# Image 0 of a two-layer fp32 block: when the sums of weight tiles run on after a pause

## The chip, the cores and the metric

The kernel runs on one core of one Trainium2 chip. The metric is the device time of one execution in microseconds; of several runs the median is taken.

## The reference

Eight images of 384 channels and 32 x 32 positions pass through two layers, in fp32. The first is a transformer block on 1024 tokens, the second a ConvNeXt-like block:

```python
# layer 0: xf is (8, 1024, 384)
qkv  = layernorm(xf, g1, beta1) @ w_qkv.T + b_qkv         # 8 heads of 48
out  = softmax(q @ k.T * 48**-0.5) @ v
x1   = out @ w_proj.T + b_proj + xf
y    = x1 + gelu(layernorm(x1, g2, beta2) @ w_fc1.T + b_fc1) @ w_fc2.T + b_fc2   # hidden 1536
# layer 1
y    = depthwise_conv_7x7(x) + dw_b
y    = layernorm(y over channels) * ln_w + ln_b
y    = gelu(y @ w1 + b1)                                  # hidden 1536
gx   = sqrt(sum over positions of y**2);  nx = gx / (mean over channels of gx + 1e-6)
y    = grn_gamma * (y * nx) + grn_beta + y
out  = x + y @ w2 + b2
```

## The kernel before, in words

Images go one after the other. TensorE does, for each: q and k, values, attention in two halves of 512 queries (for each of four pairs of heads eight steps of scores and products), the projection of each half, fc1, fc2; the depthwise convolution of an image is done on VectorE (with some taps by ScalarE and GpSimd) while TensorE works on the next image.

**Fewer matmuls through sums of tiles.** From image 1 on, q and k, w1 and (for most images) fc1, and from image 0 on fc2, are computed with a scheme that multiplies sums of weight tiles with sums of input tiles. The sums of the weights do not depend on the image. They are made once, while image 0 runs, and stored in DRAM (`s_qk`, `s_w1`, `s_fc1`, `s_fc2`, `s_w2`), from where the later products load them. Biases that a norm's or a GRN's shift adds are folded in the same time.

**The planner.** The program is recorded in Python. `Flow` holds a clock of TensorE's time at record time: each recorded group of matmuls adds its nominal length (`flow.pe`). Side work is written as generators ("chains"); a chain that yields a number is resumed when that much TensorE time has been recorded. So a yield decides behind which matmul the next instructions of the chain stand in their engine's queue. On the chip each engine takes its queue in order and waits at each instruction for its semaphores. `flow.finish` runs the rest of a chain at once.

**The side chains of image 0**, spawned before its attention except for fc1's:

- `sums_for_tiles(i)`, i = 0 and 1, starting 33 and 38 us after the spawn: three times `sums_singly`, for a third of q/k's, then w1's tiles. Both chains work in the free columns of the big `qk` tile. Each `sums_singly` issues a load of 128 x 1920 on GpSimd's queue (L1593), yields, makes 18 VectorE operations of 128 x 128 in nine groups (L1600 additions, L1603, L1637 and L1638 negations), and stores the tile by GpSimd (L1640).
- `sums_for_fc1`, after image 0's attention: two more `sums_singly`, in the tile `v`.
- `prepare(weights, False)`: fc2's sums (`forms`, L1661 to L1698; operations of 128 x 512 at L1651, L1654, L1683, L1692, L1694, stores at L1669), then `shift_through_w2` (b2's shift), then w2's sums by the same `forms`. All three use the one buffer of tag `acc`, so each load of the next waits for the last reader of the one before. `shift_through_w2` has three rounds: two loads (L1746, tile `w_gbeta`), two products on VectorE (L1752, 128 x 768), an addition (L1755), five additions (L1759), a column sum on TensorE (L294, tile `b` in a bank of the scores' pool, which has two) and a copy on ScalarE (L1763).
- `prepare(weights, True)`: b1's shift (L1725, L1727 on `pad`).

**What runs on the main path.** After the last pair of heads in each half the sums of the softmax are inverted and spread: `average` copies (L777, ScalarE), adds (L779, VectorE), moves the sums by SyncE's DMA, inverts (L786, VectorE), moves the inverses back by SyncE, and multiplies (L805, VectorE) once they have landed (tile `r`); then the projection (L760) reads the result. Then the norm before fc1: sums of channels on VectorE (L551, L554), a matmul with ones (L518, `ln_sum`), subtraction (L561), squares on ScalarE (L568), their addition (L572, L575), a matmul (L518, `ln_var`), Ln and Exp on ScalarE (L588, L589), scaling (L594). For the first half of the queries this norm runs between the attention steps of the second half.

**The pause.** When the first half has nine steps left to go, the list `quiet` gets an entry, and it is cleared behind the projection; the same again at the end of the second half. While `quiet` holds something, a chain that comes to `pause()` yields 1.0, up to 24 times, and then goes on:

```python
def pause():
    for _ in range(24):
        if quiet:
            yield 1.0
```

Chains 0 and 1 of the sums, and `shift_through_w2`, thus resume at the same TensorE time, and their groups come in turn.

**fc2** (`by_thirds`, L496) is 15 products of four matmuls each. Its inputs are made on VectorE between the products (L1083, pairs of 128 x 1024), its results are added to the image at L1080 and L1083.

Of the kernel before, what the change touches and what calls it, by code (L numbers as in the profile page):

```python
# [176 lines left out]
def block_kernel(  # L177
# [90 lines left out]
    def col(name, i):  # L268
        at, width = VEC[name]
        assert i < width  # L270
        return vec[:, at + i : at + i + 1]
# [20 lines left out]
    def column_sums(ps, i, weights, rows=slice(0, P)):  # L292

        nc.tensor.matmul(out=ps[rows, i : i + 1], lhsT=weights, rhs=ones[:, 0:1], start=True, stop=True)  # L294
        flow.pe(0.2)
# [13 lines left out]
    def columns(name):  # L309
        at, width = VEC[name]  # L310
        return vec[:, at : at + width]
# [38 lines left out]
    def chunk(w, c):  # L350
        return w[:, c * 6 * P : (c + 1) * 6 * P]
# [1227 lines left out]
            column_sums(ps, ct, t[:, ct * P : (ct + 1) * P])  # L1579
        nc.vector.tensor_tensor(bout, ps[:, :CT], columns("bproj"), ALU.add)  # L1580

    def pause():
        for _ in range(24):
            if quiet:
                yield 1.0

    def sums_singly(w, store, spare):

        shape = store.shape
        t = spare[:, : shape[1] * shape[2] * P].rearrange("p (g n o) -> p g n o", n=shape[2], o=P)
        nc.gpsimd.dma_start(out=t, in_=w.rearrange("p (g n o) -> p g n o", n=shape[2], o=P))  # L1593
        yield 13.0
        yield from pause()
        r = {n: t[:, :, i, :] for i, n in enumerate(SINGLY)}
        a12, a13, a21, a22, a23, a31, a32, a33 = (r[n] for n in (12, 13, 9, 4, 14, 0, 3, 10))

        def plus(dst, one_, other, op=ALU.add):
            nc.vector.tensor_tensor(dst, one_, other, op)  # L1600

        def minus(dst, one_, other):
            nc.vector.scalar_tensor_tensor(dst, one_, -1.0, other, ALU.mult, ALU.subtract)  # L1603

        plus(r[6], r[6], a12)
        plus(r[14], a23, a33)
        yield 0.6
        yield from pause()
        minus(r[5], r[6], a33)
        plus(r[8], r[6], a13)  # L1610
        yield 0.6
        yield from pause()
        plus(r[8], r[8], r[14], ALU.subtract)
        plus(r[11], r[14], a12, ALU.subtract)
        yield 0.6
        yield from pause()
        plus(r[13], a13, a12, ALU.subtract)
        plus(r[13], r[13], a33, ALU.subtract)
        yield 0.6
        yield from pause()  # L1620
        plus(r[7], r[14], a22, ALU.subtract)
        plus(r[4], a21, a22)
        yield 0.6
        yield from pause()
        plus(r[2], a33, r[4], ALU.subtract)
        plus(r[4], r[4], a31)
        yield 0.6
        yield from pause()
        plus(r[1], a32, r[4])
        minus(r[9], a21, a12)  # L1630
        yield 0.6
        yield from pause()
        plus(r[9], r[9], a31, ALU.subtract)
        plus(r[0], a31, r[6], ALU.subtract)
        yield 0.6
        yield from pause()
        nc.vector.tensor_scalar(r[12], a12, -1.0, None, ALU.mult)  # L1637
        nc.vector.tensor_scalar(r[14], r[14], -1.0, None, ALU.mult)  # L1638
        yield 1.0
        nc.gpsimd.dma_start(out=store, in_=t)  # L1640

    def prepare(weights, aside):
# [3 lines left out]
        def blocks(name):  # L1646
            t = one.tile([P, CT, N], F32, tag="acc", name=name).rearrange("p c n -> p (c n)")
            return t.rearrange("p (j k o) -> p j k o", j=4, o=P)
# [93 lines left out]
        def shift_through_w2():  # L1742
            for r in range(CT):
                t = blocks(f"w2_gbeta_{r}")
                for s in range(2):
                    nc.gpsimd.dma_start(out=t[:, s], in_=chunk(w2, 2 * r + s).rearrange("p (k o) -> p k o", o=P))  # L1746
                yield 14.0
                h = HT // 2
                for s in range(2):
                    yield from pause()  # L1750
                    g = columns("gbeta")[:, s * h : (s + 1) * h].unsqueeze(2).to_broadcast((P, h, P))
                    nc.vector.tensor_tensor(t[:, s], t[:, s], g, ALU.mult)  # L1752
                    yield 1.0
                yield from pause()
                nc.vector.tensor_tensor(t[:, 0], t[:, 0], t[:, 1], ALU.add)  # L1755
                for k in range(1, h):
                    yield 0.5
                    yield from pause()
                    nc.vector.tensor_tensor(t[:, 0, 0, :], t[:, 0, 0, :], t[:, 0, k, :], ALU.add)  # L1759
                yield 7.0  # L1760
                ps = ps_s.tile([P, N], F32, tag="s", name=f"b2_{r}")
                column_sums(ps, 0, t[:, 0, 0, :])
                nc.scalar.activation(b2[:, r : r + 1], ps[:, :1], AF.Identity, bias=col("b2", r), scale=1.0)  # L1763
# [7 lines left out]
        def release():  # L1771
            yield 14.0
            weights.release()

        yield from forms("fc2", wfc2, s_fc2)
        flow.spawn(release())
        yield 8.0
        yield from shift_through_w2()
        yield from forms("w2", w2, s_w2)

# [86 lines left out]
    def main():  # L1867
# [81 lines left out]
        def sums_for_tiles(i):  # L1949
            width = len(FORMS) * P  # L1950
            spare = large[0][:, (2 * NP + 2 * i) * N : (2 * NP + 2 * i + 2) * N]
            for w, store, g in ((wqkt, s_qk, i), (w1t, s_w1, i), (w1t, s_w1, i + 2)):
                yield from sums_singly(w[:, g * width : (g + 1) * width], store[:, g : g + 1], spare)
                yield 8.0

        def sums_for_fc1():
            width = len(FORMS) * P
            spare = v.rearrange("p t w -> p (t w)")
            for g in range(2):
                yield from sums_singly(wfc1t[:, g * width : (g + 1) * width], s_fc1[:, g : g + 1], spare)  # L1960
                yield 8.0
            for t in range(KT):
                nc.gpsimd.memset(v[:, t, :], 1.0)
# [122 lines left out]
        for b in range(B):  # L2086
            if b == 0:
                folding = flow.spawn(after(None, folds(weights), 8))
                preparing = flow.spawn(after(None, prepare(weights, False), 4))
                singly = [flow.spawn(after(None, sums_for_tiles(i), 33 + 5 * i)) for i in range(2)]  # L2090
                aside = flow.spawn(after(folding, prepare(weights, True), 4))
# [4 lines left out]
            if b == 0:  # L2096
                for chain in singly:
                    flow.finish(chain)
                fc1_sums = flow.spawn(after(None, sums_for_fc1(), 22.0))
                shift = flow.spawn(after(None, prepare(weights, None), 4.0))  # L2100
# [204 lines left out]
```

## Time and profile before

| | us |
|---|---|
| median of 3 runs | 3212.09 (3211.55 to 3214.67) |
| the profiled execution | 3213.02 |
| its span, first to last instruction | 3211.1 |
| TensorE busy | 3196.2 (100% of the span) |
| VectorE busy | 2550.4 (79%) |
| ScalarE busy | 1674.6 (52%) |
| GpSimd busy | 493.4 (15%) |
| mean granted TensorE clock | 0.999 |

Image 0 takes about the first 324 us: q, k and v to 67, attention to 191 with the first projection at 134.73 to 142.7, fc1 and the second projection to 269, fc2 to 324. The profile's times count from the first instruction. A row of a timeline gives start, duration, engine, source line, operation, tiles written and read, shapes, the number of instructions merged into it, and in brackets the engine's idle time before it with what ended that. TensorE's busy time contains waits too short for the profile to list.

### The profile page before, as it was taken

Reading aid. Unit: us, or ns where it says so; the run is one execution under the profiler, and the core shown is the slowest. Engines: PE = TensorE matmul, PEld = TensorE weight load, DVE = VectorE, ACT = ScalarE, POOL = GpSimd, SP = SyncE. Lnnn points to the kernel's source line nnn. Section 1 sums busy time; section 2 is a strip of 40 time slices with the busy share of each in tenths; the row PEclk is TensorE's granted clock in tenths of the full one; section 3 lists DMA queues with packets and bytes.
Section 4 is the critical chain, followed back from the end, with each engine's and each line's share of the span. In section 5 each row is a group of like instructions: output and inputs, shape, how many; then the busy total and the mean of one; then the engine's idle time right before and its main releaser. Section 6 shows DMA issues by size and latency. Waiting matters only on the chain.

```text
span 3211.1 us, 39348 instructions
## 1 busy us (share of the span) xinstructions
PE 3196.2 (100%) x14204; PEld 1402.1 (44%) x14204; DVE 2550.4 (79%) x3587; ACT 1674.6 (52%) x2363; POOL 493.4 (15%) x592
## 2 busy tenths in 40 slices
PE   9999999999999999999999999999999999999999
PEld 5344434443444434444344443444435444344454
DVE  4547788897878978789787888888887788879964
ACT  3542763456644476444754637637365374732543
POOL 2102211112111121201112011120111201200000
PEclk9999999999999999999999999999999999999999
DMA  6435742647346564456546374463743638433244
GB/s 210 155 127 170 168 90 50 162 112 165 84 88 159 123 151 92 97 142 158 115 92 124 116 186 97 81 136 106 194 92 80 148 97 200 72 81 93 55 119 111
DMA packets 206052, 393.09 MB, mean 122 GB/s; under 512 B 42656, under 2 KB 48416, under 8 KB 205472
## 3 DMA queue, kind: packets, MB, share of 16 engines
q0 software_dynamic: 79296, 163.35, 26.6%
q1 hardware_dynamic: 126272, 226.49, 23.6%
q8 instruction: 114, 1.87, 0.2%
q10 hardware_dynamic: 288, 0.71, 0.1%
q14 instruction: 82, 0.67, 0.1%
HBM read 212.98 MB, written 40.11 MB: 79 GB/s over the span
## 4 chain that ended last, share of the span: by engine, by line
PE 97%; DVE 1%; DMA 1%; ACT 0%; issue 0%; SPq 0%; DVEq 0%; ACTq 0%
PE fc L415 15%; PE s L818 13%; PE o L838 13%; PE o_p L496 11%; PE fc_p L496 11%; PE v L738 4%; PE proj L760 4%; PE h_n L467 3%; PE h_z L467 3%; PE h_x L467 3%; PE h_last L1427 2%; PE o L1378 2%; PE h L402 2%; PE qk_n L467 2%; PE qk_z L467 2%; PE qk_x L467 1%
## 5 line engine op out<-in xcount | busy, mean ns | idle before, releaser
L1244 DVE SCALAR_TENSOR_TENSOR acc<-pad,vec,acc 128x870 f32<-128x870 f32 (+8 forms) x815 | 911.0, 1157 | 2.7
L827 ACT ACTIVATE p<-s 128x1024 f32<-128x1024 f32 x512 | 524.3, 1025 | 255.2 <-PE s L818 246.9
L818 PE MATMUL s<-qk 48*64 48x512 f32 x4096 | 538.7, 591 | 0.4 <-ACT qk L660 0.2
L838 PE MATMUL o<-p,v 64*64 64x512 f32 x4096 | 535.7, 589 | 0.0
L1280 POOL DMA_DIRECT2D acc<-tap x266 | 227.0, 859 | 1354.9 <-ACT tap L1279 647.5
L415 PE MATMUL fc<-xn,fc 128*128 128x512 f32 x972 | 427.7, 594 | 0.1
L496 PE MATMUL o_p<-y,w 128*128 128x512 f32 x664 | 289.0, 592 | 0.0
L838 PEld LDWEIGHTS o<-p,v 64*64 64x64 f32 x4096 | 166.4, 132 | 273.3 <-issue 265.0
L415 PEld LDWEIGHTS fc<-xn,fc 128*128 128x128 f32 x972 | 183.1, 190 | 229.2 <-issue 220.5
L818 PEld LDWEIGHTS s<-qk 48*64 48x64 f32 x4096 | 162.3, 132 | 275.9 <-issue 213.1
L496 PE MATMUL fc_p<-qk,fc 128*128 128x512 f32 x520 | 226.6, 593 | 0.3 <-DMA qk<-qk 0.3
L1279 ACT ACTIVATE tap<-pad,vec 128x512 f32<-128x512 f32 x266 | 195.1, 736 | 2.9 <-DMA acc<-tap 2.9
L496 PEld LDWEIGHTS o_p<-y,w 128*128 128x128 f32 x664 | 125.6, 190 | 157.7 <-issue 146.4
L1244 DVE SCALAR_TENSOR_TENSOR acc_last<-pad,vec,acc_last 128x377 f32<-128x377 f32 (+24 forms) x288 | 177.2, 688 | 0.6
L496 PEld LDWEIGHTS fc_p<-qk,fc 128*128 128x128 f32 x520 | 98.2, 190 | 126.9 <-issue 117.4
L508 ACT ACTIVATE qk<-fc,bfc_f 128x512 f32<-128x512 f32 x90 | 61.6, 685 | 160.4 <-PE fc L415 160.4
L508 ACT ACTIVATE hid<-fc,bfc_f 128x512 f32<-128x512 f32 x72 | 49.4, 687 | 158.3 <-PE fc L415 158.3
L779 DVE TENSOR_TENSOR attn<-o,attn 128x512 f32<-128x512 f32 x64 | 44.1, 689 | 109.9 <-ACT attn L777 108.8
L760 PE MATMUL proj<-attn,wproj_sb 128*128 128x512 f32 x288 | 127.5, 596 | 0.7 <-DVE attn L805 0.7
L738 PE MATMUL v<-wv_sb,xn 128*128 128x384 f32 x384 | 126.8, 487 | 0.0
L991 ACT COPY pad<-x 128x512 f32<-128x512 f32 x42 | 26.3, 634 | 187.7 <-DVE x L1083 187.7
L738 PEld LDWEIGHTS v<-wv_sb,xn 128*128 128x128 f32 x384 | 72.5, 190 | 50.1 <-issue 3.4
(446 smaller groups left out, 4594.7 us busy)
## 6 DMA issues: line engine op xcount, KB each, us to landing
acc<-tap POOLq DMA_DIRECT2D x266, 256.0 KB, 3.5
fc<-s_fc SPq DMA_DIRECT2D x91, 256.0 KB, 3.0
w<-s_w SPq DMA_DIRECT2D x91, 256.0 KB, 2.7
w<-s_w SPq DMA_DIRECT2D x72, 320.0 KB, 4.2
fc<-in_wfc SPq DMA_DIRECT2D x54, 384.0 KB, 4.0
y<-y POOLq DMA_DIRECT2D x38, 512.0 KB, 6.7
qk<-qk POOLq DMA_DIRECT2D x30, 512.0 KB, 9.4
qk<-s_qk SPq DMA_DIRECT2D x42, 320.0 KB, 4.9
```

Source lines behind the costliest of these rows:

```text
L415: nc.tensor.matmul(out=ps, lhsT=lhsT(k), rhs=rhs(k)[:, half(h)], start=(k == 0), stop=(k == nk - 1))
L467: nc.tensor.matmul(out=at, lhsT=weights.at(wname, g, slot // 5)[:, slot % 5, :], rhs=rhs[n], start=first, stop=True, skip_group_check=not ...
L496: nc.tensor.matmul(out=bank, lhsT=lhsT, rhs=rhs, start=k == 0, stop=k == len(pairs) - 1)
L508: nc.scalar.activation(dst, src, function, **kw)
L738: nc.tensor.matmul(out=ps[:, :C], lhsT=xn[:, k, t * P : (t + 1) * P], rhs=wv_sb[:, k, :], start=(k == 0), stop=(k == CT - 1),)
L760: nc.tensor.matmul(out=ps, lhsT=wproj_sb[:, m, ct * P : (ct + 1) * P], rhs=attn[:, m, :], start=(m == 0), stop=(m == CT - 1),)
L818: nc.tensor.matmul(out=s[64 * i : 64 * i + 64, j, :], lhsT=kT[64 * j : 64 * j + HD, m, k0 : k0 + 64], rhs=qT[64 * j : 64 * j + HD, m, half ...
L827: nc.scalar.activation(p, s, AF.Exp)
L838: nc.tensor.matmul(out=outs[i][64 * j : 64 * j + 64, :], lhsT=v[keys, t, at : at + 64], rhs=p[keys, j, :], start=(t == 0), stop=(t == KT - 1),
L1244: nc.vector.scalar_tensor_tensor(dst, window, tap, dst, ALU.mult, ALU.add)
L1279: nc.scalar.mul(t.rearrange("p (h w) -> p h w", w=W), window, tap)
L1280: nc.gpsimd.dma_start(out=acc[:, ct, half(h)], in_=t, accum_op=ALU.add)
```

## The change

Four edits, all in the planning of image 0's side chains:

- `pause` takes a number. A chain that was in fact held yields this number once more when the pause ends, so that it resumes later. `sums_singly` hands it on: 11 for chain 0 of the q/k and w1 sums, 16 for chain 1. For fc1's sums and in `shift_through_w2` it is 0, a yield that lets other due chains go first.
- `sums_singly` yields 10 us instead of 13 between its load and its first operation.
- `shift_through_w2` yields 12 us instead of 14 between its loads and its first product.
- Between fc2's sums and `shift_through_w2` 3 us are yielded instead of 8.

```diff
-    def pause():
+    def pause(behind=0):
+        paused = False
         for _ in range(24):
             if quiet:
+                paused = True
                 yield 1.0
-
-    def sums_singly(w, store, spare):
+        if paused:
+            yield behind
+
+    def sums_singly(w, store, spare, behind=0):
...
         nc.gpsimd.dma_start(out=t, in_=w.rearrange("p (g n o) -> p g n o", n=shape[2], o=P))
-        yield 13.0
-        yield from pause()
+        yield 10.0
+        yield from pause(behind)
...
         plus(r[6], r[6], a12)
         plus(r[14], a23, a33)
         yield 0.6
-        yield from pause()
+        yield from pause(behind)
...
                     nc.gpsimd.dma_start(out=t[:, s], in_=chunk(w2, 2 * r + s).rearrange("p (k o) -> p k o", o=P))
-                yield 14.0
+                yield 12.0
...
         yield from forms("fc2", wfc2, s_fc2)
         flow.spawn(release())
-        yield 8.0
+        yield 3.0
         yield from shift_through_w2()
...
             for w, store, g in ((wqkt, s_qk, i), (w1t, s_w1, i), (w1t, s_w1, i + 2)):
-                yield from sums_singly(w[:, g * width : (g + 1) * width], store[:, g : g + 1], spare)
+                yield from sums_singly(w[:, g * width : (g + 1) * width], store[:, g : g + 1], spare, 11.0 + 5.0 * i)
                 yield 8.0
```

The same replacement of `pause()` by `pause(behind)` is made at each of the nine groups of `sums_singly`.

## The prediction

> **What bounds the kernel now.** I read the page first, then TensorE's waits over the whole span, then the busy time by stage, then the timelines of TensorE and VectorE around the two stages that stood out.
>
> ```profile
> span 3211.1 us, 39348 instructions
> PE 3196.2 (100%) x14204; PEld 1402.1 (44%) x14204; DVE 2550.4 (79%) x3587; ACT 1674.6 (52%) x2363; POOL 493.4 (15%) x592
> PE 97%; DVE 1%; DMA 1%; ACT 0%; issue 0%; SPq 0%; DVEq 0%; ACTq 0%
> ```
>
> TensorE is the bound: it is idle for 14.9 us in all. The change moves VectorE and DMA work of image 0 and removes no instruction, so it can gain only what TensorE loses in image 0. TensorE's waits name those losses:
>
> ```profile
> PE fc_p L496 <- issue: 2.1, 1, 2.1
> PE ln_var L518 <- DVE ln_sq L575: 2.1, 1, 2.1
> ...
> PE proj L760 <- DVE attn L805: 0.7, 1, 0.7
> ...
> PE fc_p L496 <- DVE hid L1083: 0.3, 1, 0.3
> ...
> PE s L818 <- ACT p L827: 0.2, 1, 0.2
> ```
>
> By stage (stretch, length, busy time of PE, PEld, DVE, ACT, POOL, then granted clock, DMA share, GB/s):
>
> ```profile
> 143.00:168.00 25.00, 22.74 (x178) 7.19 (x174) 19.84 (x59) 14.11 (x18) 2.61 (x5) 0.93 0.23 83
> 270.00:325.00 55.00, 52.53 (x124) 22.84 (x123) 47.77 (x63) 5.06 (x9) 13.80 (x28) 1.00 0.56 181
> ```
>
> In 143 to 168 us TensorE is idle for 2.26 us and its clock is 0.93; in 270 to 325 us it is idle for 2.47 us. VectorE is busy for 79% and 87% of them. The timelines (start, duration) say who is late:
>
> ```profile
> 157.23 1.04 PE L838 MATMUL o<-p,v 64*64 64x512 f32 x8
> 160.35 1.12 PE L518 MATMUL ln_var<-ln_sq,ones 128*128 128x512 f32 x2 [2.08 <-DVE ln_sq L575]
> 161.41 1.42 PE L818 MATMUL s<-qk 48*64 48x512 f32 x8
> 162.59 1.95 PE L838 MATMUL o<-p,v 64*64 64x512 f32 x8
> 164.29 1.62 PE L818 MATMUL s<-qk 48*64 48x512 f32 x8
> ...
> 292.98 3.74 PE L496 MATMUL fc_p<-fc_e,fc 128*128 128x512 f32 x8 [2.12 <-issue]
> ```
> ```profile
> 159.61 0.69 DVE L575 TENSOR_TENSOR ln_sq<-ln_sq,ln_sq 128x512 f32<-128x512 f32 x1
> ...
> 291.66 1.22 DVE L1083 TENSOR_TENSOR fc_e<-hid 128x1024 f32<-128x1024 f32 x1
> ```
>
> L575 ends at 160.30 and the variance matmul starts at 160.35. The "issue" of the second stall is VectorE too: fc_e ends at 292.88, its matmul starts at 292.98.
>
> **What the change moves.** The order of instructions of both programs differs in image 0 alone; each engine issues the same instructions, and SyncE's order is the same.
>
> *First norm.* Before, both w1 sum chains stand between L554 (ends 144.83) and L575: 36 operations of 128x128 (L1600, L1603, L1637, L1638) and two L1752 of 0.95, rows that take about 11 us of VectorE. Now the first chain's first 16 operations, 4 of the second and both L1752 stand ahead of the pause, behind the pad work that ends at 107.95, where VectorE idled until 109.79 and from 110.5 to 119.5. Two negations come behind L575, the other 14 behind L594. Between L554 and L575 stay L1755 (0.95), five L1759 (0.28), L779, three L561 (1.88), L786, L572. So L561 can start when its sum matmul ends (147.4) instead of 150.57. ScalarE then puts its three squares (0.63) between exponentials (1.02, one per 1.72 us): 0.63 + 1.02 = 1.65 fits. The third square ends near 153.6, L575 near 154.4; TensorE asks at 157.8. Gains:
> - the wait: after L838 a 128-row matmul follows 0.97 later (145.28 to 146.25), so 160.35 - (157.23 + 0.97) = 2.15;
> - the slow clock behind it: 25 us x (1 - 0.93) = 1.75;
> - the scores at 152.88, which waited for an exponential held up behind the late squares: 152.88 - (151.66 + 0.86) = 0.36.
>
> The Trainium skill (TensorE: Matmul & The Clock Gate, Part 1) has the clock halve after about 3.4 us idle. By that rule a gap of 2.1 us costs no clock; this trace disagrees, since the half-rate rows at 161.41 to 165.84 follow a gap of 2.08.
>
> *fc2.* Before, w2's sums stand among the operations that make f, h and e: from the L1080 at 276.55 to the end of fc_e at 292.88 are 16.33 us. Six of them now run ahead of fc2 (L1654, L1651, L1683: 3.86 us); the two negations come in instead (0.67). 16.33 - 3.86 + 0.67 = 13.14. That L1080 starts 0.21 after its matmuls (276.34), and TensorE asks for fc_e after products 2 to 5, 4 x 3.43 = 13.73 us: 13.14 + 0.21 + 0.10 for the handover = 13.45, in time by 0.28. The stall of 292.98 - (279.78 + 3 x 3.43) = 2.91 (the 0.35 at 288.87 is inside it) goes. Its cover is thin: each further VectorE operation of 0.7 us costs some 0.4.
>
> Sum: 2.15 + 1.75 + 0.36 + 2.91 = 7.17 us.
>
> *At nothing, with the cover.*
> - First two (q, k) chains: VectorE starts them when the load lands (78.58) as before, but 24 operations (4.45 us per 18: 5.9) now stand before the L779 at 82.27: it moves to about 84.4. Its sums land later (86.3 before; up to 5.4 us after issue as at 98.72), and the pads, fc2's sums and the L779 at 98.01 move by 0 to 2 us. Cover: the projection at 134.73.
> - The second w1 load landed at 114.71; four operations that need it now stand ahead of the L779 at 109.79. GpSimd's queue issues it after the second q/k store, which moves from 98.65 ahead of fc2's last three stores, so at 102 to 104 instead of 104.58: landing 112 to 115 by the old latency, L779 at 114 to 117. Behind it wait its sums, L786 (120.16) and two more rounds of SyncE's divisors. The last L805 ends at 134.60; the projection's third matmul needs it at 134.73 + 2 x 0.86 = 136.44, so 1.8 us of delay is free. I take 0, bounds 0 and +1.
> - b2's column sum (TensorE, 0.3) moves to just behind the variance. It takes a score bank, so the next scores wait for the exponential that ended at 158.55, 0.3 earlier now; they start near 159. ScalarE's next exponential ends near 161.9, asked for at 162.6. At nothing, bounds 0 and +0.7.
> - b2's second and third loads, w1's later stores and w2's loads are issued 4 to 9 us sooner on GpSimd, and take their usual 3.4 to 10 us; those for b2 and w1 land 2 us or more ahead of their first reader. w2's last block lands near 260, when VectorE comes to it, 8 us before the latest start (268.3) that still frees VectorE for the L1080 near 272.2. At the second b2 sum ScalarE's table load waits about 1.5 us longer; the gelu behind it frees a bank needed 5 us later.
> - fc1's shorter load wait (10 for 13): the first landed at 205.12 and is used near 216, the second at 245.59, used at 251.56 before and near 247 now, with its load some 4 us sooner.
> - 0.71 at the projection (206.27) stays: its divisors land late beside the same load.
>
> The profiled execution took 3213.02 (span 3211.1, 1.9 around it), 0.93 over the median of 3212.09. 3213.02 - 7.17 = 3205.85; from the median 3204.9.
>
> **Rivals.**
> 1. *The clock.* The profiled run had one half-rate stretch here; if the median one had none, 1.75 is not to be gained: 3212.1 - 5.4 = 3206.7. For: the three runs spread over 3.1 us, and the 0.35 + 2.12 gap before 292.98 left the clock at 1.00. Against: the rows at 161.41. The Trainium skill (TensorE: Matmul & The Clock Gate, Part 1) gives this time too, by its 3.4 us; it also says that the activity window runs freely, so that its phase differs from run to run, which no run here can show yet.
> 2. *fc_e stays late.* The margin is 0.28. If VectorE comes into fc2 late (w2's loads landing after 268), or one more operation slips in, most of 2.91 stays: 3212.1 - 4.3 = 3207.8. Against: eight microseconds of slack on the loads.
> 3. *The norm stays late*, because ScalarE rather than VectorE delays the variance, or b2's bank does: only 2.91 is gained, 3209.2.
> 4. *No change*: the loads set the order, TensorE finds the same stalls: 3212.
> 5. *Slower: the second w1 load holds VectorE.* With this load in front, L779 and the first half's divisors queue behind it. With 1.84 to spare, L786 may come at 122.0 instead of 120.16; its sums take up to 3.8 us (192.70 to 196.53) from the end of L779, so L779 must start by 117.5, and 2.2 us of operations stand between the load and L779. So it decides from a landing at 115.3 on; each us beyond is a us of idle TensorE at the projection, and with 1.75 of clock the gain is eaten up at about 121. At 126: 10.7 + 1.75 - 7.17 = +5.3, 3217. For: the landing that I expect is within 3 us of that point. Against: 126 is over 20 us from the issue, where the slowest load of this size took 10.1 (104.58 to 114.71).
>
> **Numbers.** Both stalls go with the clock 0.45 (3204.9); rival 1 0.18; rival 2 0.13; rival 3 0.09; rival 4 0.06; rival 5 0.05; others 0.04. The range takes in rivals 1 to 3: up to 3209.2, and down to 3203.2, where the clock also fell at 292.98 (another 1.7). The bound of 0.2% (6.4 us) is about what a measurement of this kernel can tell from no change; my likeliest case lies only 0.7 beyond it, rivals 1 to 4 are within. So 0.46 faster, 0.48 within, 0.06 slower.
>
> **What would show it.** In the changed profile: no ln_var wait on L575 in image 0 and a clock of 1.00 there; L575 ending near 154; no gap before the fc_p that reads fc_e; the image-0 values (L738 at 324.03) near 316.9. Wrong would be: a TensorE gap at the first projection (134 to 137), at the scores behind b2, or fc_p still waiting.

## The result and the profile after

| | before | after |
|---|---|---|
| median of 15 runs each, us | 3212.08 (3210.25 to 3214.67) | 3205.24 (3203.77 to 3206.25) |
| the profiled execution | 3213.02 | 3206.18 |
| its span | 3211.1 | 3204.4 |

The changed kernel is faster by 6.84 us by the medians and by 6.84 in the profiled executions; the ratio is 0.9979 [0.9971, 0.9986], a gain of 0.2% that is clear of the noise. The forecast was 3204.9 (3203.2 to 3209.2). Lines beyond 1590 have numbers higher by 4 in the changed kernel (L1752 is L1756, L1640 is L1644); in the experiments below they are shifted by 2 to 8.

The page of the changed kernel (busy times, then the chain of waits by engine):

```profile
span 3204.4 us, 39347 instructions
PE 3194.1 (100%) x14204; PEld 1404.3 (44%) x14204; DVE 2552.8 (80%) x3587; ACT 1673.8 (52%) x2363; POOL 493.1 (15%) x592
PE 98%; DMA 1%; DVE 0%; ACT 0%; issue 0%; SPq 0%; POOL 0%; DVEq 0%; ACTq 0%; POOLq 0%
```

TensorE's idle time is 10.3 us instead of 14.9. Its waits over the whole span (total, times, longest):

```profile
PE proj L760 <- DVE attn L805: 1.1, 1, 1.1
...
PE ln_var L1808 <- ACT ln L1825: 1.0, 1, 1.0
PE ln_var L532 <- DVE acc L1244: 0.7, 1, 0.7
```

The waits at L518 and L496 have left the list. The wait at the projection has grown from 0.7. By stage (stretch, length, PE, PEld, DVE, ACT, POOL, clock, DMA share, GB/s) the two stretches shown before have no idle TensorE and full clock:

```profile
143.00:168.00 25.00, 25.00 (x215) 8.76 (x218) 15.14 (x38) 16.53 (x21) 2.55 (x5) 1.00 0.30 112
...
270.00:325.00 55.00, 55.00 (x136) 25.50 (x135) 50.87 (x66) 6.86 (x12) 9.83 (x19) 1.00 0.64 210
```

The timeline of TensorE, then of VectorE, at the two places:

```profile
157.28 1.04 PE L838 MATMUL o<-p,v 64*64 64x512 f32 x8
158.25 1.12 PE L518 MATMUL ln_var<-ln_sq,ones 128*128 128x512 f32 x2
159.21 0.28 PE L294 MATMUL b<-ones,w_gbeta 128*128 128x1 f32 x2
159.42 1.09 PE L818 MATMUL s<-qk 48*64 48x512 f32 x8
...
286.34 3.60 PE L496 MATMUL fc_p<-fc_e,fc 128*128 128x512 f32 x8
```
```profile
154.00 0.69 DVE L575 TENSOR_TENSOR ln_sq<-ln_sq,ln_sq 128x512 f32<-128x512 f32 x1 [1.03 <-ACT ln_sq L568]
...
284.75 2.35 DVE L1083 TENSOR_TENSOR fc_e<-hid 128x1024 f32<-128x1024 f32 x2
```

L575 now ends at 154.69, 3.6 us before TensorE comes to the variance; b2's column sum and the scores behind it run at the usual pace. The matmul that reads fc_e has no gap before it.

Where the 6.7 us of span lie, from the starts of five TensorE instructions in the two profiles:

| stretch | before | after | difference | forecast |
|---|---|---|---|---|
| start to first projection | 134.73 | 135.19 | +0.46 | 0 |
| to the variance (L518) | 25.63 | 23.06 | -2.57 | -2.51 |
| to the second projection | 43.32 | 41.27 | -2.05 | -1.75 (clock) |
| to fc2's first matmul | 65.80 | 66.23 | +0.43 | 0 |
| to image 0's values (324.03, 317.24) | 54.55 | 51.50 | -3.05 | -2.91 |
| to the end | 2887.11 | 2887.16 | +0.05 | 0 |

The +0.46 is there at 61 us already (the bias matmul of the values at 61.04 and 61.49), so it comes from the loads at the start and not from the edits. The +0.43 is the projection's wait, 1.14 for 0.71. Single profiles scatter in the first and the last row: over the profiles of this document the first projection starts between 134.33 and 135.51, and the last row lies between 2885.36 and 2888.15. The stretches between them are the ones to compare.

### The profile page after: what moved, and what is told of

Its sections match the earlier page's. It is cut to its first block, busy times and chain, and to the rows that moved or that the text cites. A ratio compares the mean times of both kernels' runs of the same rounds, so it can differ in the third digit from the quotient of the medians.

```text
span 3204.4 us, 39347 instructions
## 1 busy us (share of the span) xinstructions
PE 3194.1 (100%) x14204; PEld 1404.3 (44%) x14204; DVE 2552.8 (80%) x3587; ACT 1673.8 (52%) x2363; POOL 493.1 (15%) x592
## 4 chain that ended last, share of the span: by engine, by line
PE 98%; DMA 1%; DVE 0%; ACT 0%; issue 0%; SPq 0%; POOL 0%; DVEq 0%; ACTq 0%; POOLq 0%
PE fc L415 15%; PE s L818 13%; PE o L838 13%; PE o_p L496 11%; PE fc_p L496 11%; PE v L738 4%; PE proj L760 4%; PE h_n L467 3%; PE h_x L467 3%; PE h_z L467 3%; PE h_last L1427 2%; PE o L1378 2%; PE h L402 2%; PE qk_n L467 2%; PE qk_z L467 2%; PE qk_x L467 2%
## 5 line engine op out<-in xcount | busy, mean ns | idle before, releaser
L496 PE MATMUL o_p<-y,w 128*128 128x512 f32 x664 | 289.0, 593 | 0.0
L496 PE MATMUL fc_p<-qk,fc 128*128 128x512 f32 x520 | 226.4, 593 | 0.1
L496 PEld LDWEIGHTS o_p<-y,w 128*128 128x128 f32 x664 | 125.7, 190 | 157.6 <-issue 146.2
L496 PEld LDWEIGHTS fc_p<-qk,fc 128*128 128x128 f32 x520 | 98.4, 190 | 126.4 <-issue 117.6
L508 ACT ACTIVATE qk<-fc,bfc_f 128x512 f32<-128x512 f32 x90 | 61.6, 684 | 160.7 <-PE fc L415 160.7
L508 ACT ACTIVATE hid<-fc,bfc_f 128x512 f32<-128x512 f32 x72 | 49.3, 686 | 155.4 <-PE fc L415 155.4
L779 DVE TENSOR_TENSOR attn<-o,attn 128x512 f32<-128x512 f32 x64 | 44.1, 690 | 101.7 <-ACT attn L777 100.5
```

What stands on the lines that cost most here:

```text
L496: nc.tensor.matmul(out=bank, lhsT=lhsT, rhs=rhs, start=k == 0, stop=k == len(pairs) - 1)
L508: nc.scalar.activation(dst, src, function, **kw)
```

## The experiments

**One half of the edits at a time.** The first two kernels undo the edits to the one kind of chain or to the other.

`norm_part`, the changed kernel with the w2 shift's yields as before:

```diff
-                yield 12.0
+                yield 14.0
...
-        yield 3.0
+        yield 8.0
         yield from shift_through_w2()
```

> Only the edits to the q/k and w1 sums (pause with 11 and 16, 10 us instead of 13); the w2 shift keeps 14 and 8. Theory A (two stalls of TensorE, each cured by VectorE's order at its place): both L1752 (0.87 each) return between L554 and L575 but the 36 operations of 128x128 do not; L561 starts near 147.9, L575 ends near 154.5, no ln_var wait, clock 1.00; fc_p waits 2.1 and 0.3 as before. Gain 4.26: 3207.8. Theory B (the half-rate stretch was an accident of one run): no ln_var wait, but only 2.5 gained: 3209.6. Theory C (the sums' edits alone bring all or nothing): 3205.2 or 3212.1.

Measured 3212.21 (3209.02 to 3213.91), ratio to before 0.9999 [0.999, 1.0008]: no gain, although the wait at the norm is gone. TensorE's waits in this kernel, and the stretch around fc2's gap (columns as above):

```profile
PE fc_p L496 <- issue: 2.1, 1, 2.1
PE fc L415 <- ACT hid L508: 1.5, 1, 1.5
```
```profile
287.07:290.48 3.41, 1.28 (x4) 0.36 (x3) 3.41 (x6) 0.59 (x1) 0.04 (x1) 1.00 0.44 137
290.48:293.89 3.41, 3.41 (x6) 1.33 (x5) 3.40 (x3) 0.00 (x0) 1.03 (x2) 0.50 0.41 154
```

Two things show in the rows. The half-rate stretch did not go; in this profile it stands behind the gap at fc2, which in the profile of before had left the clock at 1.00. And a wait of 1.5 stands at fc1, in place of the projection's 0.71: the gelu L508 comes late (below). So theory A was right on the wait and wrong to give the clock to this one gap. From the first projection to the end of image 0 this profile is still 2.2 us shorter than that of before; the rest of the median's missing gain is not accounted for, beyond the scatter of the first and last rows (0.78 and 0.64 longer here).

`w2_part`, the changed kernel with the sums' edits undone:

```diff
-        if paused:
-            yield behind
...
-        yield 10.0
+        yield 13.0
```

> Only the edits to the w2 shift (12 for 14, 3 for 8); the sums keep 13 and a pause without a further yield. Theory A: no wait at fc_p (2.91). At the norm the 36 operations of 128x128 stay in front of L575, but both L1752 now stand ahead of the pause, so L575 ends 1.7 us earlier (160.30 to 158.6) and the gap at ln_var shrinks from 2.15 to 0.4, too short for a slower clock: 3212.1 - 2.91 - 1.75 - 1.75 = 3205.7, nearly all of the gain by the w2 edits alone. Theory A' (any gap halves the clock): 3207.4. Theory D (each half cures its own stall only): ln_var waits 2.1 as before: 3209.2.

Measured 3207.77 (3206.49 to 3209.70), 0.9988 [0.9979, 0.9997]. The gap at the norm was 0.62 (0.4 expected) with full clock, as theory A has it and theory D does not: the w2 edits alone take most of the norm's wait. But fc_p still waited, and the cause is a row that I had not looked for. GpSimd's, VectorE's and TensorE's timelines of this kernel (here L1965 is the memset of v, L1694 and L1696 are the two negations):

```profile
278.15 3.11 POOL L1965 MEMSET v<- 128x407 f32 x8
```
```profile
278.98 0.68 DVE L1083 TENSOR_TENSOR x<-x,fc_p 128x512 f32<-128x512 f32 x1
279.57 1.97 DVE L1694 TENSOR_SCALAR w_a<-w_a 128x512 f32<-128x512 f32 x1
281.46 0.41 DVE L1696 TENSOR_SCALAR w_a<-w_a 128x512 f32<-128x512 f32 x1
```
```profile
288.31 3.67 PE L496 MATMUL fc_p<-fc_e,fc 128*128 128x512 f32 x8 [1.10 <-ACT fc_n L1073]
```

The bracket of the matmul names a copy of ScalarE, but that ended at 287.82; the first of the two fc_e operations ends at 288.21. The first negation took 1.97 instead of 0.42 and ended 0.28 after the memsets (281.26); the TENSOR_TENSOR beside them took its usual 0.68. Without the sums' edits the fc1 store lands later, and the eight memsets that wait for it run at 278 instead of 266. `memset_late` moves them alone:

```diff
                 yield 8.0
+            yield 14.0
             for t in range(KT):
                 nc.gpsimd.memset(v[:, t, :], 1.0)
```

> The kernel with only the edits of the w2 shift, and GpSimd's eight memsets of v recorded 14 us later, behind the w2 sums' negation stores. Theory M (the negation L1692 took 1.97 instead of 0.42 because a memset of GpSimd ran beside it, and that 1.55 of VectorE is what made fc_e late): both negations take 0.42, fc_e is 0.4 early, no wait at fc_p instead of 1.10: 3207.8 - 1.1 = 3206.7. Rival (w2's sums came into fc2 late, or the order of VectorE differs): the wait stays at 1.1, 3207.8.

Measured 3206.34 (3205.34 to 3207.95), and VectorE's timeline:

```profile
279.44 0.42 DVE L1694 TENSOR_SCALAR w_a<-w_a 128x512 f32<-128x512 f32 x1
279.77 0.42 DVE L1696 TENSOR_SCALAR w_a<-w_a 128x512 f32<-128x512 f32 x1
```

Both negations are back at 0.42, the wait at fc_p is gone, and 1.4 us with it (1.34 in the profiles, from fc2's first matmul to image 1's values): theory M. The Trainium skill (SBUF — State Buffer, Who interferes with whom) says that VectorE's tensor_scalar in its two-port mode and a GpSimd instruction exclude each other, the later one blocked until the first ends, while a tensor_tensor is not hindered by a GpSimd instruction that only writes. The rows agree: 1.97 against 0.42, and 0.68 against 0.68. The negation ended only behind the last of the eight memsets, so here it was held by more than one instruction.

`g_alone` has only the one yield of 3 for 8:

```diff
         flow.spawn(release())
-        yield 8.0
+        yield 3.0
         yield from shift_through_w2()
```

> Only 3 for 8 ahead of the w2 shift. Theory A: one L1752 ahead of the pause: L575 ends near 159.4, ln_var gap 1.28; three of the six w2 operations ahead of fc2, so the stretch from the L1080 to the end of fc_e is 16.33 - 1.93 + 0.67 = 15.07, fc_e late by 15.07 + 0.31 - 13.73 = 1.65. 3212.1 - 0.87 - 1.26 = 3210.0 where a gap of 1.28 halves the clock, 3208.2 where it does not. Rival (fc2 is late or in time as a whole, not by the microsecond): fc_p waits 2.9 or 0.

Measured 3207.74 (3206.39 to 3209.14), with a gap of 1.02 at the norm (1.28 expected), 1.49 at fc_p (1.65 expected; 1.66 by the starts of the matmuls, see `neg4`) and full clock. About half of each gap is left, and about half of the gain is had: fc2 and the norm go by the microsecond of VectorE's queue. One changed number brings 4.2 us (3211.89 for the kernel before in these comparisons).

**The pause's further yield.** `no_behind` keeps the three shorter yields and leaves the pause as it was:

```diff
-        if paused:
-            yield behind
```

> All shorter yields (10, 12, 3), but the pause without a further yield. Theory A: chain 1's last operations, 12 of 128x128 and two negations of chain 0, return between L554 and L575, some 3 us of VectorE, 1.9 of it ahead of L561, which moves from 147.9 to 149.2; L575 ends near 156.0, TensorE asks at 158.7: no wait. fc2 as in the changed kernel. 3205.2, no difference from the changed kernel: the further yield is worth nothing by itself. Rival (the chains that go on behind the pause make the norm late, as the change's words suggest): a ln_var wait of 1 to 2 and the slow clock come back: 3207 to 3209.

Measured 3204.09 (3203.55 to 3207.06), so the edit that gives the change its name seems to cost time. It was run again beside the changed kernel, on one chip:

> The changed kernel once more, on the chip of the three runs that follow, for a direct comparison: 3205.2 by every theory.

> The kernel with the shorter yields and no further yield at the pause's end, once more beside the changed kernel. Theory S (11 and 16 push the last w1 sums and their store into the second half's divisors, and that is what the projection's wait of 1.14 is): about 1.1 less than the changed kernel, 3204.1, and no wait of L760. Rival (the first comparison was chance): 3205.2.

Measured 3205.23 (3203.95 to 3206.68) for the changed kernel and 3203.96 (3202.57 to 3205.22) without the further yield, 1.3 less. VectorE's timeline of `no_behind2`, then of the changed kernel, then of the kernel before, at the second half's last divisors:

```profile
189.80 0.20 DVE L786 RECIPROCAL inv<-sums 128x8 f32<-128x8 f32 x1 [1.37 <-DMA sums<-attn]
...
195.71 0.69 DVE L805 TENSOR_TENSOR attn<-attn,r 128x512 f32<-128x512 f32 x1 [3.03 <-DMA r<-back]
```
```profile
192.35 0.20 DVE L786 RECIPROCAL inv<-sums 128x8 f32<-128x8 f32 x1 [3.24 <-DMA sums<-attn]
...
201.79 0.69 DVE L805 TENSOR_TENSOR attn<-attn,r 128x512 f32<-128x512 f32 x1 [8.43 <-DMA r<-back]
```
```profile
196.53 0.20 DVE L786 RECIPROCAL inv<-sums 128x8 f32<-128x8 f32 x1 [3.26 <-DMA sums<-attn]
...
205.52 0.69 DVE L805 TENSOR_TENSOR attn<-attn,r 128x512 f32<-128x512 f32 x1 [8.01 <-DMA r<-back]
```

With 11 and 16 the last w1 sums end at 187.7 and their store is issued at 188.03, beside the move of the softmax's sums, for which VectorE then waits 3.24 instead of 1.37; without them the last store is issued at 181.02. The further yield did not bring the store there: in the kernel before, the store (192.19) and a wait of 3.26 stand at the same place, some 4 us later like everything around them. `w2_part` has no further yield and 13 between load and first operation, and its store is issued at 188.94. So it is the 10 for 13 that moves the store out of the way, and the further yield that holds it back.

There is a second price. fc1's result is written over the big `qk` tile, so the first gelu waits for that last store too; a second profile of the changed kernel (`after2`) has no wait at the projection, but this on ScalarE and TensorE:

```profile
192.97 1.28 ACT L508 ACT_TABLE_LOAD   x1 [5.24 <-DMA s_w<-qk]
```
```profile
195.01 5.42 PE L415 MATMUL fc<-xn,fc 128*128 128x512 f32 x12 [0.91 <-ACT hid L508]
```

This is also the 1.5 of `norm_part`. In `no_behind2` the table load comes at 187.22 and nothing waits. From the first variance to fc2's first matmul the profiles have 109.1 us before, of which 1.7 is the slow clock, 107.5 and 107.1 in the changed kernel (`after2` second), and 105.7 in both runs without the further yield. By these rows it costs 1.4 to 1.8, in line with the medians.

**The load beside the divisors.** `fc1_behind` is the changed kernel with fc1's first load behind the last L805, through a small GpSimd copy of its result:

```diff
-        nc.gpsimd.dma_start(out=t, in_=w...)
-        yield 10.0
+        if late:
+            yield late
+            seen_attn = small.tile([P, 8], F32, tag="inv", name="behind_attn")
+            nc.gpsimd.tensor_copy(seen_attn, attn[:, ORDER[-1], :8])
+        nc.gpsimd.dma_start(out=t, in_=w...)
+        yield 10.0 - late
```

> The changed kernel with the first load for fc1's sums behind the last L805 of the second half (a GpSimd copy of 128x8 of its result stands ahead of the load), so near 199 instead of 194.5. Theory L (the divisors' last loads land 5.9 us after their issue because this load of 128x1920 runs beside them; without it 2.3 us, as in the first half): L805 near 198.7, no wait of L760: 1.1 less than the changed kernel, 3204.1. Theory S alone (the store and the late sums): the last L805 still comes at 201 to 202, the wait stays near 1.1.

Measured 3203.61 (3203.34 to 3203.86), the lowest median of all, 0.9973 [0.9962, 0.9983]. VectorE's timeline:

```profile
192.44 0.20 DVE L786 RECIPROCAL inv<-sums 128x8 f32<-128x8 f32 x1 [3.42 <-DMA sums<-attn]
...
198.28 0.69 DVE L805 TENSOR_TENSOR attn<-attn,r 128x512 f32<-128x512 f32 x1 [5.54 <-DMA r<-back]
```

The sums are as late as in the changed kernel, but the divisors' last loads, issued at 195.85, are through at 198.28 and not 6 us after their issue: theory L. The gain in time is not explained by it. This profile still has the gelu's wait (1.06), and from the variance to fc2 it takes 107.0 us, only 0.1 to 0.5 less than the changed kernel's two profiles; the 1.6 of the median stays open. The intervals of the three ratios (0.9973, 0.9975 for `no_behind2`, 0.9979) overlap; the order of the three rests on the runs of one chip.

**The margin of fc_e.** `neg4` puts four more negations ahead of fc_e:

```diff
             nc.vector.tensor_scalar(a23, a23, -1.0, None, ALU.mult)
+            if name == "w2":
+                for _ in range(4):
+                    nc.vector.tensor_scalar(a23, a23, -1.0, None, ALU.mult)
```

> The changed kernel with four more negations of 128x512 (in place, one behind the other, 0.33 to 0.44 each, 1.3 to 1.8 in all) between the w2 sums' two negations and fc_e. Theory A (fc_e's margin is 0.27 and every further microsecond of VectorE is TensorE's): fc_p waits 1.05 to 1.5, clock 1.00: 3206.3 to 3206.7. Rival (there is slack that the sum did not count): no wait, 3205.2.

Measured 3207.59 (3206.60 to 3209.64); the wait at fc_p is 1.40, in the range expected. The four operations hold VectorE for 1.85 (the next operation starts at 282.23 instead of 280.38). A listed wait counts from the modelled end of the matmul before; by the starts the matmul that reads fc_e is late by 288.75 - (276.88 + 3 x 3.43) = 1.58, so the margin is 0.27, as forecast. `w2_part` gives the same: 1.55 more on VectorE, late by 288.31 - (276.74 + 3 x 3.43) = 1.28. The median is 0.9 above the expectation. The profiled execution, the slowest of the eleven, has another 1.27 at the first projection, where the second w1 load was issued at 109.97 instead of 106.18 and landed at 116.46 instead of 112.97; whether the others have it is not known.

**The second w1 load.** `w1_late6` records that load 6 us later and leaves its sums in place:

```diff
+        if late:
+            yield late
         nc.gpsimd.dma_start(out=t, in_=w...)
-        yield 10.0
+        yield 10.0 - late
```

> The changed kernel with the second w1 load recorded 6 us later, so that it stands behind the w2 shift's loads and the pads' two folds on GpSimd's queue, while its sums stay where they are. It is issued near 112 instead of 106.2 and lands at 118 to 120 instead of 112.97. Prediction's rival 5 (from a landing near 115.3 + 0.46 on, each microsecond is one of idle TensorE at the first projection): a wait of L760 for L805 of 2.5 to 4.5, with or without a half-rate stretch: 3207.7 to 3211. Rival (the projection has more cover than I counted): no wait before a landing of 120, 3205.2.

Measured 3207.27 (3206.26 to 3209.25). VectorE's, then TensorE's timeline:

```profile
121.05 1.02 DVE L1606 TENSOR_TENSOR qk<-qk 128x128 f32<-128x128 f32 x4 [5.24 <-DMA qk<-in_w1t]
121.99 0.68 DVE L779 TENSOR_TENSOR attn<-o,attn 128x512 f32<-128x512 f32 x1
...
124.64 0.20 DVE L786 RECIPROCAL inv<-sums 128x8 f32<-128x8 f32 x1 [1.37 <-DMA sums<-attn]
```
```profile
137.86 2.41 PE L760 MATMUL proj<-attn,wproj_sb 128*128 128x512 f32 x5 [1.42 <-DVE attn L805]
```

The load landed at 121.03. Rival 5's rule asks for 5.3 us of idle TensorE there and the run has 1.42: the mechanism is real, but there was more cover. L779 at 119.03 (`norm_part`) brings no wait, at 121.28 (`neg4`) 1.27, at 121.99 1.42. By these two waits the limit for its start is 120.0 to 120.6, not 118.

**The clock.** `gap16` and `gap20` put operations in place between L572 and L575 of the first norm, so that the variance is late by a chosen time:

```diff
         nc.vector.tensor_tensor(squares[0], squares[0], squares[1], ALU.add)
+        if name == "ln2_0" and h == 0:
+            for _ in range(16):   # 20 in gap20
+                nc.vector.tensor_scalar(squares[0], squares[0], 1.0, None, ALU.mult)
```

> The changed kernel with 16 VectorE operations in place (0.44 each) between L572 and L575 of the first norm: L575 ends near 160.6, a ln_var gap of about 2.4. Theory W (the clock is set in fixed stretches of 3.413 us, whose grid runs on through the whole execution; a stretch in which TensorE was idle for about half halves the next one): a gap of 2.4 falls by half a stretch or more into one of them with a chance of 2.4/3.41 = 0.7, so some 7 of 10 executions lose 2.4 + 1.7, the others 2.4: two heaps near 3207.6 and 3209.3, median 3209.3; a half-rate stretch in the profile starts within 3.4 us of the gap's end and lasts 3.413. Theory P (any gap over 2 us halves the clock): all at 3209.3. Theory R (only about 3.4 us idle halve it): all at 3207.6.

> As before with 20 such operations: L575 ends near 162.4, a gap of about 4.2. Theory W: one stretch at least always holds more than half a stretch of idle time, so every execution loses 1.7 at least, and about 1 in 4 loses it twice: 3205.2 + 4.2 + 1.7 = 3211.1, some at 3212.8. Theory P and theory R: 3211.1, all alike.

Measured for `gap16`: a gap of 2.88, median 3209.35, mean clock 0.999 in all 11 runs; for `gap20`: a gap of 4.73, median 3211.80, 0.999 in 6 runs (median 3211.53) and 0.998 in 5 (3212.68). Theory R is out: with 2.88 alone the median would be 3208.1 and the clock full. By theory W the longer gap of 2.88 brings a half-rate stretch in about 0.84 of the executions (2.88 / 3.413), and 4.73 always brings one and often a second, as seen. The two heaps expected of `gap16` are not there; with 0.84 that happens by chance in one of seven such sets of 11. Theory P fails on the before-kernel itself, below. The stretches along the grid, busy time of TensorE behind the length, the clock third from the end; `before` first, then `gap20`:

```profile
158.62:162.04 3.42, 1.69 (x10) 0.65 (x14) 1.57 (x4) 0.52 (x1) 1.13 (x2) 1.00 0.62 252
162.04:165.45 3.41, 3.41 (x24) 0.80 (x13) 2.35 (x4) 2.40 (x4) 0.00 (x0) 0.50 0.79 324
...
288.33:291.74 3.41, 2.18 (x5) 0.68 (x4) 3.41 (x5) 0.59 (x1) 0.19 (x1) 1.00 0.55 213
291.74:295.15 3.41, 2.17 (x5) 0.98 (x6) 3.41 (x6) 0.00 (x0) 1.07 (x2) 1.00 0.44 142
```
```profile
156.51:159.92 3.41, 1.70 (x16) 0.30 (x8) 3.13 (x9) 1.29 (x2) 0.00 (x0) 1.00 0.00 0
159.92:163.33 3.41, 0.39 (x1) 0.30 (x2) 3.00 (x8) 0.00 (x0) 0.00 (x0) 1.00 0.00 0
163.33:166.74 3.41, 3.41 (x16) 1.38 (x18) 0.28 (x1) 1.47 (x3) 1.68 (x3) 0.50 0.65 268
```

In `before` the gap of 2.1 at the norm lay by 1.73 in one stretch of the grid, and the next one ran at half rate; the gap of 2.1 at fc2 fell across a border, 1.23 and 1.24 idle, and cost no clock. In `norm_part` the gap at fc2 lay by 2.13 in one stretch, and the next was at half rate.

## Why the prediction was right, step by step

- **The norm's wait, 2.15 + 0.36.** Right: 2.57 less up to the variance. L575 ends at 154.69 (154.4 forecast), the third square at 153.96 (153.6). Not all of the named operations had to go: the w2 edits alone, two operations of 0.95, leave 0.62, and the yields without the pause's edit leave none.
- **The slow clock, 1.75.** Right in size, but booked to the norm's gap alone. In the profile of before the stretch did follow that gap; `norm_part` shows that the other gap brings one too when the first is closed. It goes because the change closes both. Of 94 comparison runs of the kernel before, 30 had a mean clock of 1.000 (median 3211.3), 63 one of 0.999 (3212.4) and one 0.998; of the changed kernel's 11 runs (`after2`) only two had 0.999. (The mean also holds the half rate behind the last matmul, so 0.999 points to a stretch in the middle but does not prove it.) Rival 1 was half right: the stretch is a matter of phase, but most executions have one. By the medians 6.84 - (2.57 + 3.05 - 0.43) = 1.65 is left for the clock; half of a stretch of 3.413 is 1.71.
- **fc2, 2.91.** Right: 3.05, and by the way forecast: the six named operations run at 263.83 to 267.78, ahead of fc2, and only the two negations come in. The margin of 0.28 was right too: 0.27 by two kernels.
- **Rival 2 (fc_e stays late)** did not happen in the changed kernel, but did in `w2_part`, by a way that the working did not have: a memset on GpSimd beside a negation. Here the memsets run at 266.08 to 269.16, 9.7 us ahead of the negation at 278.88.
- **At nothing: the second w1 load.** It was issued at 106.18 (102 to 104 forecast), landed at 112.97 (112 to 115), and L779 came at 117.91, later than forecast and at the limit of 117.5 + 0.46 that rival 5 gave. No wait came of it, because the limit was wrong: the move of the sums was taken at 3.8 us from the end of L779, a row of the second half where a store runs beside it, and takes 2.0 here (122.67 to 124.64 in `w1_late6`). With 2.0 in its place the limit comes to 119.8, near the 120.0 to 120.6 measured. L779 was late through the sums ahead of it (L786 at 107.42 for 104.13), not through the load.
- **At nothing: b2 and the w2 loads.** b2's sum costs nothing; the exponential behind it ends at 161.94 (161.9 forecast). The last w2 block landed at 263.71, not near 260, and VectorE waited 2.70 for it, still 4.5 us ahead of the limit of 268.3.
- **"0.71 at the projection stays."** It stayed as a mechanism: 1.14 in this profile, and in `after2` none, with 0.91 at the first gelu instead. The 0.43 more is scatter of fc1's load beside the divisors: the last L805 starts 7.28 us after that load's issue (194.51), 6.86 before (198.66), and kernels without the further yield but with the old load yield wait 0.67 (`g_alone`), 0.93 (`w2_part`) and 1.02 (`memset_late`). What the working missed is that the wait need not stay. The shorter yields alone take the w1 sums' last store out of the way of the softmax's sums and of the first gelu, and the further yield puts that back. The working priced the edits only together and so could not tell that the further yield costs 1.15 and 1.27 by the two pairs of medians and brings nothing that the shorter yields do not.
- **The total, 7.17.** Measured 6.84. The norm's and fc2's terms came out within 0.15 of the forecast, so this is not a sum of errors that cancel; the 0.43 at the projection is the largest miss.

## What to carry to other kernels

Price a delayed side chain by what stands behind its last instruction, the store included, and by who reuses its memory: here a further yield, which the norm did not need, kept a store beside the next critical transfer. Where two stalls can each slow the clock, book the clock's loss to both together. And before moving work on VectorE, look which of its single-input operations it brings beside GpSimd's.

## What the runs showed of the hardware

- **The clock's grid.** The half-rate stretches inside an execution last 3.413 us, and their borders lie on a grid that runs on: with a step of 3.4133, 162.04 and 3210.14 in `before` are 893.0 steps apart, 290.48 and 3208.87 in `norm_part` 855.0. Whether a stretch is slow goes with the one before: 1.60 (`gap16`), 1.73, 2.13 and 3.02 us without matmuls were followed by half rate; 1.49 (`g_alone`) and less were not, and neither were 1.71 in `gap20` and 1.64 at the end of `gap16`. So the idle time alone does not decide. The 1.60 of `gap16` has 0.28 of a one-column sum (L294) beside it, and in `w1_late6` 0.96 idle with 0.94 of 64x1 column sums in the same stretch was followed by half rate, so thin matmuls seem to count as idle; that was not tried by itself. The Trainium skill (TensorE: Matmul & The Clock Gate, Part 1) has the freely running window of 3413 ns, and the runs agree; it asks for an idle window of about 3.4 us, and here about half of one was enough.
- **A broadcast beside a large load.** The last divisor loads took 6.0 us from issue (195.76) to use beside a load of 128 x 1920, 2.4 without it (`fc1_behind`). Their own issue mattered little: where the large load was issued first, their reader started 0.4 to 1.1 us after it had landed (205.12 and 205.52 in `before`, 200.23 and 201.36 in `after2`).
- **A negation beside a memset** took 1.97 instead of 0.42 (`w2_part`, `memset_late`), while a TENSOR_TENSOR beside the same memsets kept its 0.68.
